# Expert layers of a routed network as seven block products instead of eight

## The chip, the core and the metric

The kernel runs on one core of a Trainium2 chip. Its engines work side by side, each through its own queue of instructions in order: TensorE (PE; its weight loads are shown apart as PEld), VectorE (DVE), ScalarE (ACT), GpSimd (POOL), and SyncE (SP), which here starts transfers. The metric is the device time of one execution in microseconds. Before the change the median of three runs is 1369.45 us (1367.98 to 1369.69).

## The reference

Four parts follow one another: a layer of experts, a linear attention in blocks, a conditioned attention, and two layers of local attention with a feed-forward part. The change touches the first alone. `x` has 4 x 512 tokens of 256 values, and there are eight experts.

```python
gate = xn @ wg_W + wg_b + (genre_embed @ gg_W + gg_b)
gate_w = jax.nn.softmax(gate, axis=-1)
topk_w, topk_i = jax.lax.top_k(gate_w, TOP_K)            # TOP_K = 2
cw = jnp.sum(jax.nn.one_hot(topk_i, E) * topk_w[..., None], axis=-2)
h1 = jax.nn.relu(jnp.einsum('bsh,ehm->bsem', x, W1) + b1)    # 256 -> 512
h2 = jax.nn.relu(jnp.einsum('bsem,emn->bsen', h1, W2) + b2)  # 512 -> 512
out_e = jnp.einsum('bsen,enh->bseh', h2, W3) + b3            # 512 -> 256
return jnp.einsum('bseh,bse->bsh', out_e, cw)
```

Everything is in 32-bit floats.

## The kernel before

Each token goes only to its two best experts. A first stretch computes the gate, sorts the 4096 pairs of token and expert by expert, and cuts them into slots of 256 or 128 rows; a slot has one expert, whose number is read from memory. `SLOTS` fixes the order: sizes 128, 256, 256, 128, 256, 256, then three times 128, 256, 256, 256, then 128, 256, 256, 128 (slots 0 to 21, of which fifteen have 256 rows), and two more of 128 that run only if they are needed. Rows that no token fills are written like the others, but to row 0 of the table `ys`, which nobody reads.

A slot `j` goes through these steps:

- `loads(j)`: SP starts three transfers of the expert's weights: `w1` (with its biases), `w2`, `w3`. There are two buffers for each.
- `gather(j)`: POOL issues one indirect transfer for each 128 rows, which fetches the tokens `xb`; TensorE transposes them into the bank `pxb`; ACT or DVE, in turn, copies them to `xbT`.
- `layer` with `w1`: result `h1`, 512 hidden units in four blocks of 128 partitions, tokens along the free side. For 256 rows that is 8 matmuls of 256 columns (two chunks of 128 inputs for each block). Two blocks share a PSUM bank, and ACT and DVE take turns at adding the bias and the relu (`relu`).
- `layer` with `w2`: result `h2`, from `h1`, 16 matmuls of 256 columns.
- `last(j)`: 8 matmuls with `w3` (4 for 128 rows) into `po`, one DVE addition of the bias into `ob`, and for each 128 rows an indirect transfer by POOL that scatters the rows to `ys`. A scatter waits until the scatter before it has landed.

The loop over the slots shifts these against one another: layer one of slot `j`, the last layer of slot `j - 1`, the loads, the gather and the transposes of slot `j + 1`, layer two of slot `j`. Except where code asks for program order (`PE.in_order`, `tc.keep_in_program_order`), a planner in the build sets the order on each engine from estimated times. Weights of later stages are loaded one by one in between (`later`), and POOL already adds bias rows (`crows`) to the residual tiles (`xres`) in this stage and clears a tile (`v`). When all slots are done, the results are read back from `ys`, weighted and summed into `y`, four tiles that nothing uses before.

PSUM has eight banks. In this stage four are for the layers (`mm`), two for transposes (`tp`), two for `po` and small products (`acc`). For the reader of the profile: a 32-bit matmul appears as two records, each with a weight load of its own; so the 16 matmuls of layer two of a 256-row slot are 32 records.

Of the kernel before, what the change touches and what calls it, by code (L numbers as in the profile page):

```python
# [12 lines left out]
F32 = mybir.dt.float32  # L13
I32 = mybir.dt.int32
AF = mybir.ActivationFunctionType
ALU = mybir.AluOpType
# [3 lines left out]
B, S, H = 4, 512, 256  # L20
NT = S // 128
# [21 lines left out]
NRARE = 2  # L43
NROWT = 2 * NPAIR + NHALF
NHI = 2 * NROWT
MCONST = (128, 128 + NE, 2 * NE, 2, NE * NE, NHI, 2 * B * NT, 64, NE)
NMC = sum(MCONST)


# [18 lines left out]
def adaln_attn_ffn_kernel(ctx: ExitStack, tc: tile.TileContext, a: dict, out: bass.AP):  # L68
# [50 lines left out]
    def acct(name):  # L119
        return bank("acc" if "acc" in ps_now else "mm", name)  # L120
# [1041 lines left out]
    with ExitStack() as abc:  # L1162
# [5 lines left out]


        with ExitStack() as moe:  # L1170
            moe.enter_context(banks("ps0", mm=4, tp=2, acc=2))
            xp = moe.enter_context(tc.tile_pool(name="xp", bufs=1, reuse_waits="tile"))
            ew = moe.enter_context(tc.tile_pool(name="ew", bufs=2, reuse_waits="tile"))
            hp = moe.enter_context(tc.tile_pool(name="hp", bufs=2, reuse_waits="tile"))
# [13 lines left out]
            for n in MCONST:  # L1188
                parts.append(mc[:, at : at + n])
                at += n  # L1190
            mtri, mtiles, mthr, mslot, mlow, miota, mtok, mfold, mwt = parts


            ys = dr.tile([1 + 2 * B * S, H], F32, tag="ys", name="ys")
            xall = a["x"].rearrange("b s h -> (b s) h")


# [8 lines left out]
            with PE.in_order():  # L1206

                warm = acct("pwarm")
                for _ in range(8):
                    PE.matmul(warm[:, 0:128], ident, ident, start=True, stop=True)  # L1210
                xT2s = [ew.tile([128, 4, ME], F32, tag="w2", name="xT") for _ in range(2)]
                xTs = [xT2s[b // 2][:, b % 2 * 2 + c, :] for b in range(B) for c in range(2)]

                for n, b in enumerate((0, 2, 3, 1)):
                    for c in range(2):
                        pt = mmt("pxt")
                        for t in range(NT):
                            PE.transpose(pt[:, t * 128 : (t + 1) * 128], xres[b][:, t, c * 128 : (c + 1) * 128], ident)
                        pinned(nc.vector.tensor_copy(xTs[2 * b + c], pt))
                    sq = hp.tile([128, NT, H], F32, tag="h2", name="sq")  # L1220
                    for t in range(NT):
                        nc.scalar.activation(sq[:, t, :], xres[b][:, t, :], AF.Square,
                                             accum_out=ss[:, b * NT + t : b * NT + t + 1])
                    if n == 1:

                        for c in range(2):
                            pinned(nc.vector.tensor_scalar_mul(wgs[:, c, 0:NE], wg[:, c, :], col("rms", c)))
                        csB = xp.tile([CD, B, 128], F32, tag="csB", name="csB")
                        pinned(nc.vector.tensor_copy(csB, csT.unsqueeze(2).to_broadcast([CD, B, 128])))
                        gb0 = xp.tile([128, NE], F32, tag="gb0", name="gb0")  # L1230
                        pinned(nc.vector.tensor_add(gb0, grow[:, 0, :], grow[:, 1, :]))
                pgb = acct("pgb")
                for b in range(B):
                    PE.matmul(pgb[:, b * NE : (b + 1) * NE], csB[:, b, :], ggw, start=True, stop=True)
                pg = acct("pg")
                for c in range(2):
                    for b in range(B):
                        PE.matmul(pg[32 * b : 32 * b + 32, :], wgs[:, c, :], xTs[2 * b + c],
                                  start=(c == 0), stop=(c == 1))
# [159 lines left out]
            pmap2 = acct("pmap2")  # L1399
            for q in range(2):  # L1400
                PE.matmul(pmap2[64 * q : 64 * q + 64, :NROWT], mfold, half_map[:, :, q], start=True, stop=True)
            goal = xp.tile([128, NROWT], I32, tag="goal", name="goal")
            nc.vector.tensor_copy(goal, pmap2[:, :NROWT])
            rowtok = xp.tile([128, NROWT], I32, tag="rowtok", name="rowtok")
            nc.vector.tensor_scalar(rowtok, pmap2[:, :NROWT], -1.0, 0.0, ALU.add, ALU.max)
            nc.vector.tensor_single_scalar(rowtok, rowtok, B * S - 1, op=ALU.bitwise_and)


            def busy(n):
# [7 lines left out]

            def relu(dst, src, bias):
                if turn[0]:
                    nc.scalar.activation(dst, src, AF.Relu, bias=bias)  # L1420
                else:
                    nc.vector.tensor_scalar(dst, src, bias, 0.0, ALU.add, ALU.max)  # L1422


            def place(kind, i):
# [11 lines left out]
                d.w3 = ew.tile([128, 5, H], F32, tag="w3", name="w3")  # L1437
                nc.sync.dma_start(d.w3, we[:, 8 + 6 * ME :].rearrange("p (c m) -> p c m", m=H))

            def gather(j, d):  # L1440
                xb = hp.tile([128, 2, H], F32, tag="xb", name="xb", bufs=3)
                for i in range(d.n):
                    r = place(d.n, SLOTS[j][0]) + i
                    nc.gpsimd.indirect_dma_start(
                        out=xb[:, i, :], out_offset=None, in_=xall,
                        in_offset=bass.IndirectOffsetOnAxis(ap=rowtok[:, r : r + 1], axis=0))
                n = d.n * 128
                pt = tpt("pxb")
                with PE.in_order():
                    for c in range(2):  # L1450
                        for i in range(d.n):
                            PE.transpose(pt[:, c * n + i * 128 : c * n + (i + 1) * 128],
                                         xb[:, i, c * 128 : (c + 1) * 128], ident)
                xbT = hp.tile([128, 2, 256], F32, tag="xbT", name="xbT")
                evac(xbT[:, :, 0:n], pt[:, : 2 * n].rearrange("p (c t) -> p c t", t=n))
                d.xbT = xbT

            def layer(d, src, tag, w, bias):
                n = d.n * 128
# [14 lines left out]
                        relu(dst[:, m, 0:n], ps[:, i * n : (i + 1) * n], d.w1[:, bias + m : bias + m + 1])  # L1474
                return dst

            def last(j, d):
                ps = acct("po")
                for i in range(d.n):
                    mm(ps[:, i * H : (i + 1) * H],  # L1480
                       [(d.h2[:, c, i * 128 : (i + 1) * 128], d.w3[:, c, :]) for c in range(4)])
                ob = hp.tile([128, 2, H], F32, tag="ob", name="ob", bufs=3)
                nc.vector.tensor_tensor(
                    ob[:, 0 : d.n, :], ps[:, : d.n * H].rearrange("p (i h) -> p i h", h=H),
                    d.w3[:, 4, :].unsqueeze(1).to_broadcast([128, d.n, H]), ALU.add)
                for i in range(d.n):
                    r = place(d.n, SLOTS[j][0]) + i
                    nc.gpsimd.indirect_dma_start(
                        out=ys, out_offset=bass.IndirectOffsetOnAxis(ap=goal[:, r : r + 1], axis=0),
                        in_=ob[:, i, :], in_offset=None)  # L1490


            later = {
# [5 lines left out]
            cond_weights(wp, lambda name, load: later.update({name: load}))  # L1499
            cw_ = {}  # L1500

            ds = [SimpleNamespace() for _ in SLOTS]
            loads(0, ds[0])
            gather(0, ds[0])
            often, rare = ds[:-NRARE], range(len(ds) - NRARE, len(ds))
            for j, d in enumerate(often):
                if j == len(often) - 1:
                    aside = conditions(cw_, wp)
                    next(aside)
                if j == len(often) - 2:  # L1510
                    halves = nc.values_load(nhalf[0:1, 0:1], min_val=0, max_val=2 * NE)
                if j == 1:
                    weights()
                h1 = layer(d, d.xbT, "h1", d.w1[:, 8:].rearrange("p (c m) -> p c m", m=ME), 0)
                if j:
                    last(j - 1, ds[j - 1])
                if j + 1 < len(often):
                    loads(j + 1, ds[j + 1])
                    gather(j + 1, ds[j + 1])
                    if j > 1 and later:  # L1520
                        name, behind[0] = next(iter(later)), True
                        cw_[name] = later.pop(name)()
                        behind[0] = False
                d.h2 = layer(d, h1, "h2", d.w2, 4)
            last(len(often) - 1, often[-1])

            next(aside)
            busy(1)
            with tc.If(halves > NHALF - NRARE):
                for j in rare:  # L1530
                    d = ds[j]
                    loads(j, d)
                    gather(j, d)
                    h1 = layer(d, d.xbT, "h1", d.w1[:, 8:].rearrange("p (c m) -> p c m", m=ME), 0)
                    d.h2 = layer(d, h1, "h2", d.w2, 4)
                    last(j, d)
            next(aside)
            busy(4)
            run(aside)
# [210 lines left out]
def _shape_constants():  # L1750
# [20 lines left out]
         np.tile((e[None, :] <= e[:, None]).reshape(-1), (128, 1)).astype(f), np.tile(np.arange(NHI), (128, 1)).astype(f),  # L1771
         (np.arange(2 * B * NT)[None, :] * 128 + p[:, None] + 1).astype(f),
         (p[:, None] % 64 == np.arange(64)[None, :]).astype(f),
         np.tile(np.where(e == NE - 1, 1 - NE, 1), (128, 1)).astype(f)], axis=1)

    pos = np.arange(S, dtype=f)
    inv = f(10000.0) ** np.repeat(np.arange(0, H, 2, dtype=f) / f(H), 2)
# [94 lines left out]
```

## Time and profile before

| | |
|---|---|
| median of three runs | 1369.45 us |
| the profiled execution, its own time | 1364.1 us |
| its span, first to last instruction | 1362.3 us |
| mean granted clock of TensorE | 0.990 |

The execution in stages, with each engine's busy time in each stretch. The columns are the stretch, its length, and for each engine its busy time and number of instructions; then the clock granted to TensorE, the share of DMA time and what it moved.

```profile
0.00:20.00 20.00, 12.18 (x76) 9.70 (x76) 9.37 (x25) 10.76 (x36) 3.62 (x14) 0.95 0.39 121
20.00:42.00 22.00, 11.87 (x85) 8.45 (x86) 14.81 (x56) 4.78 (x18) 3.19 (x4) 0.66 0.57 217
140.00:180.00 40.00, 40.00 (x218) 35.83 (x217) 8.60 (x18) 5.78 (x14) 12.00 (x14) 1.00 0.70 242
300.00:320.00 20.00, 19.18 (x95) 12.52 (x94) 6.87 (x22) 5.10 (x9) 3.07 (x5) 1.00 0.11 35
```

The five numbers with an x in parentheses are PE, PEld, DVE, ACT and POOL. The slots run from 42 to about 314 us; before 42 lies the gate and the sorting, after it the other three parts. In the slots the weights arrive at some 200 to 270 GB/s. Groups of instructions in later views are named by line, engine, operation and tiles (`out<-in`), with busy time, mean duration in ns, and the idle time before them with what ended it. Line 82 is the helper that issues every matmul, so groups are told apart by their tiles: `ph<-xbT,w` is layer one, `ph<-h,w` layer two, `po<-w,h` the last layer.

### The profile page before, as it was taken

What the parts mean: (1) busy time and instruction counts of PE and PEld (TensorE: products, weight loads), DVE (VectorE), ACT (ScalarE), POOL (GpSimd) and SP (SyncE); (2) the same over time, 40 slices, a digit from 0 to 9 for tenths busy, and PEclk for the clock granted to TensorE, in tenths of its full rate; (3) what the DMA queues carried; (4) which work ended last, traced back from release to release, by engine and by line L of the source; (5) the groups of instructions that cost most, each with busy time, mean ns of one, the idle gap of its engine ahead of it and who ended that gap; (6) DMA issues with size and microseconds to landing.
All of it is one profiled execution on the core that took longest, in us unless ns stands there. A gap on an engine that the chain in (4) does not pass through costs nothing.

```text
span 1362.3 us, 25766 instructions
## 1 busy us (share of the span) xinstructions
PE 1302.8 (96%) x10700; PEld 850.1 (62%) x10700; DVE 645.4 (47%) x1343; ACT 563.9 (41%) x1111; POOL 227.1 (17%) x223
## 2 busy tenths in 40 slices
PE   5899999998999999999999999999999998999998
PEld 4788888884666644444435665766555566667654
DVE  6222212125777743332226777764362767765421
ACT  4111111125555456565655646552223565463111
POOL 1324322211000020010103322100030312210010
PEclk7999999999999999999999999999999999999999
DMA  4577666644000000000201011211001011011000
GB/s 135 205 244 280 228 231 240 211 155 136 1 1 1 0 1 1 1 0 1 90 5 67 13 29 37 81 42 25 24 1 43 24 34 26 19 42 50 20 20 26
DMA packets 43110, 95.02 MB, mean 70 GB/s; under 512 B 9568, under 2 KB 25192, under 8 KB 40168
## 3 DMA queue, kind: packets, MB, share of 16 engines
q1 hardware_dynamic: 37560, 81.81, 18.1%
q0 software_dynamic: 3792, 10.24, 2.2%
q8 instruction: 88, 1.44, 0.4%
q10 hardware_dynamic: 1632, 1.21, 0.3%
q14 instruction: 38, 0.31, 0.1%
HBM read 83.95 MB, written 7.21 MB: 67 GB/s over the span
## 4 chain that ended last, share of the span: by engine, by line
PE 83%; DVE 7%; ACT 6%; issue 2%; DMA 1%; POOL 0%; POOLq 0%; SPq 0%; DVEq 0%; ACTq 0%
PE ph L82 14%; PE pdq L82 10%; PE sc L82 6%; PE pfy L82 6%; PE pug L82 5%; PE pua L82 5%; PE pv L82 5%; PE po L82 5%; PE pdy L82 4%; PE pn L82 3%; PE pz L82 2%; PE pds L82 2%; ACT p L685 2%; PE pqk L82 1%; PE pur L82 1%
## 5 line engine op out<-in xcount | busy, mean ns | idle before, releaser
L82 PE MATMUL pdq<-wqkv,yT 128*128 128x512 f32 x384 | 171.2, 596 | 6.0 <-ACT yT L613 4.1
L425 ACT ACTIVATE cex<-sc 128x512 f32<-128x512 f32 x256 | 131.8, 607 | 84.5 <-PE sc L82 84.4
L82 PE MATMUL ph<-h,w 128*128 128x256 f32 (+1 forms) x704 | 132.8, 346 | 1.6 <-DVE h L1422 1.6
L639 POOL TENSOR_TENSOR qr<-t,t 128x512 f32<-128x512 f32 x64 | 81.3, 1271 | 297.4 <-DVE t L636 282.8
L82 PEld LDWEIGHTS pdq<-wqkv,yT 128*128 128x128 f32 x384 | 71.4, 190 | 90.3 <-issue 76.9
L82 PEld LDWEIGHTS ph<-h,w 128*128 128x128 f32 x704 | 116.1, 191 | 13.7 <-DVE h L1422 1.9
L1420 ACT ACTIVATE h<-ph,w 128x256 f32<-128x256 f32 (+1 forms) x88 | 35.3, 437 | 190.9 <-PE ph L82 130.5
L1422 DVE TENSOR_SCALAR h<-ph,w 128x256 f32<-128x256 f32 (+1 forms) x88 | 36.1, 438 | 161.1 <-PE ph L82 102.6
L685 ACT ACTIVATE p<-pds,ss 128x192 f32<-128x192 f32 (+1 forms) x256 | 82.3, 434 | 12.5 <-PE pds L82 11.2
L82 PE MATMUL sc<-qm,kT 32*128 32x512 f32 x512 | 86.8, 639 | 0.0
L629 ACT ACTIVATE sq<-pdq 128x512 f32<-128x512 f32 x64 | 38.4, 601 | 97.1 <-POOL qr L639 50.2
L82 PE MATMUL pug<-hT,w 128*128 128x512 f32 x160 | 75.9, 597 | 0.0
L82 PE MATMUL pua<-hT,w 128*128 128x512 f32 x160 | 75.2, 592 | 0.0
L82 PE MATMUL ph<-xbT,w 128*128 128x256 f32 (+1 forms) x352 | 68.7, 347 | 0.5 <-ACT xbT L127 0.5
L82 PE MATMUL po<-w,h 128*128 128x256 f32 x296 | 67.6, 379 | 0.0
L395 POOL TENSOR_SCALAR fterm<-vw,faT 128x256 f32<-128x256 f32 x16 | 14.6, 922 | 312.1 <-DVE cr L385 259.6
L789 ACT ACTIVATE gl<-pug,cols 128x512 f32<-128x512 f32 x40 | 27.3, 687 | 86.5 <-PE pug L82 86.4
L82 PEld LDWEIGHTS ph<-xbT,w 128*128 128x128 f32 x352 | 58.5, 191 | 7.2 <-ACT xbT L127 0.7
L82 PE MATMUL pfy<-w,uA 128*128 128x256 f32 x256 | 61.2, 382 | 0.0
L82 PEld LDWEIGHTS pn<-p,v 64*64 64x64 f32 x1792 | 44.1, 136 | 27.4 <-issue 10.1
L82 PE MATMUL pv<-cex,v 128*32 128x512 f32 x512 | 61.2, 597 | 0.0
L82 PEld LDWEIGHTS po<-w,h 128*128 128x128 f32 x296 | 55.7, 190 | 8.1 <-ACT h L1420 0.9
(304 smaller groups left out, 2182.7 us busy)
## 6 DMA issues: line engine op xcount, KB each, us to landing
w<-in_moe_w_dram SPq DMA_DIRECT2D x22, 1024.0 KB
w<-in_moe_w_dram SPq DMA_DIRECT2D x22, 640.0 KB
w<-in_moe_w_dram SPq DMA_DIRECT2D x22, 516.0 KB
zb<-rows SPq DMA_DIRECT2D x32, 256.0 KB
g<-ys SPq DMA_DIRECT2D x6, 512.0 KB
wqkv<-in_f_wqkv_dram SPq DMA_DIRECT2D x2, 1536.0 KB
w<-in_f_w_dram SPq DMA_DIRECT2D x2, 1408.0 KB
out_dram<-yc SPq DMA_DIRECT2D x16, 128.0 KB
```

Of the source, the lines that this page charges most:

```text
L82: cls._queue(nc.tensor.matmul(*args, **kw))
L395: nc.gpsimd.tensor_scalar_mul(fterm[:, t, :], vw, W["faT"][:, t, b : b + 1])
L425: nc.scalar.activation(ex[:, i, :], pss[2 * j + i], AF.Exp, scale=CHD**-0.5)
L629: nc.scalar.activation(sq, p3, AF.Square)
L639: nc.gpsimd.tensor_tensor(qr_t[:, s], t1, t2, ALU.add)
L685: nc.scalar.activation(p[:, at : at + n], pss[j // 2][r][:, at % 384 : at % 384 + n], AF.Exp, scale=d.ss[:, j, 1, 2 * c + r : 2 * c + r + 1])
L789: nc.scalar.activation(gl, pg, AF.Gelu, bias=col("bg", l * (NU + 1) + i))
L1420: nc.scalar.activation(dst, src, AF.Relu, bias=bias)
L1422: nc.vector.tensor_scalar(dst, src, bias, 0.0, ALU.add, ALU.max)
```

## The change

For fourteen of the fifteen 256-row slots (all but slot 1) layers one and two are computed in another way. Weights are cut into 2 x 2 blocks (two halves of the inputs, two halves of the 512 outputs), the tokens' matrix also (two halves of the inputs, 128 and 128 rows). A product of such matrices takes eight block products; by a known identity (Strassen's, in Winograd's form) seven are enough, of sums of blocks on each side, whose results are then summed.

- The weights' side: `weight_sums`, four additions on POOL for each layer, 256 columns for layer one and 512 for layer two, into the `y` tiles, which are free in this stage. They are made for slot `j + 1` during slot `j`.
- The tokens' side: `token_sums`, four additions on DVE for each layer, on 128 columns for layer one and 256 for layer two. One operand of each is read from PSUM: for layer one the bank of the transposes; for layer two a tile of two banks (`act`), into which ACT writes three of the four blocks of `h1` a second time (`copies`).
- The products: `layer_few`, in the order p1, p2, p6, p5, p7, p4, p3. Each is two matmuls of 128 columns in layer one and four in layer two, so 14 and 28 instead of 8 and 16 of 256 columns.
- The results: ACT copies p1; DVE makes seven additions for each layer, each with a PSUM operand; ACT applies bias and relu to each of the four blocks in two halves of 128 columns.

Around this: PSUM is split into `mm` 4, `tp` 1, `acc` 1, `act` 2. The gather is cut into `fetch` (the transfers, now for slot `j + 2`) and `turn_tokens` (the transposes; the copy is always ACT's). All TensorE instructions of the slots, and those of the helpers, keep program order. The second scatter of a slot is issued after the first weight sums. Rows without a token get rows of their own behind the table (`maside`, `goalf`).

```diff
-            moe.enter_context(banks("ps0", mm=4, tp=2, acc=2))
+            moe.enter_context(banks("ps0", mm=4, tp=1, acc=1, act=2))
...
+            def turn_tokens(d):
+                n = d.n * 128
+                pt = tpt("pxb")
...
+                pinned(nc.scalar.copy(dst, src))
+                if d.few:
+                    d.t1 = token_sums(d.xbT, src)
...
+            def weight_sums(s, w):
...
+                pinned(nc.gpsimd.tensor_tensor(s[0], a21, a22, ALU.add))
+                pinned(nc.gpsimd.tensor_tensor(s[1], s[0], a11, ALU.subtract))
+                pinned(nc.gpsimd.tensor_tensor(s[2], a11, a21, ALU.subtract))
+                pinned(nc.gpsimd.tensor_tensor(s[3], a12, s[1], ALU.subtract))
...
+                b11, b12, b21, b22 = blocks(src)
+                _, c12, c21, c22 = blocks(src if psum is None else psum)
...
+                pinned(nc.vector.tensor_tensor(t[:, 0], c12, b11, ALU.subtract))
+                pinned(nc.vector.tensor_tensor(t[:, 1], c22, t[:, 0], ALU.subtract))
+                pinned(nc.vector.tensor_tensor(t[:, 2], c22, b12, ALU.subtract))
+                pinned(nc.vector.tensor_tensor(t[:, 3], c21, t[:, 1], ALU.subtract))
...
+                def block(i0, j0, out, p, other):
+                    plus(out, p, other)
+                    for m in range(2):
+                        pinned(nc.scalar.activation(
+                            dst[:, 2 * i0 + m, 128 * j0 : 128 * j0 + 128], out[:, m], AF.Relu,
+                            bias=d.w1[:, bias + 2 * i0 + m : bias + 2 * i0 + m + 1]))
+                    if copies is not None and (i0, j0) != (0, 0):
+                        for m in range(2):
+                            pinned(nc.scalar.activation(
+                                copies[:, 2 * i0 + m, 128 * j0 : 128 * j0 + 128], out[:, m], AF.Relu,
+                                bias=d.w1[:, bias + 2 * i0 + m : bias + 2 * i0 + m + 1]))
...
+                p1 = product(whole(0, 0), src[:, 0:n, 0:128])
+                pinned(nc.scalar.copy(e1, p1))
+                p2 = product(whole(0, 1), src[:, n : 2 * n, 0:128])
+                block(0, 0, e15, p2, e1)
+                p6 = product(summed(1), t[:, 1])
+                plus(e16, p6, e1)
+                p5 = product(summed(0), t[:, 0])
+                plus(e15, p5, e16)
+                p7 = product(summed(2), t[:, 2])
+                plus(e17, p7, e16)
+                block(1, 1, e16, p5, e17)
+                p4 = product(whole(1, 1), t[:, 3])
+                block(1, 0, e1, p4, e17)
+                p3 = product(summed(3), src[:, n : 2 * n, 128:256])
+                block(0, 1, e15, p3, e15)
...
+                with PE.in_order():
+                    if d.few:
+                        copies = both_banks()
+                        h1 = layer_few(d, d.xbT, d.t1, "h1", w1, d.s1, 0, copies)
+                        t2 = token_sums(h1, copies)
+                    else:
+                        h1 = layer(d, d.xbT, "h1", w1, 0)
+                    if j + 1 < len(often):
+                        loads(j + 1, after)
...
+                    if after.few and j + 2 < len(often):
+                        fetch(j + 2, ds[j + 2])
+                    if j:
+                        last(j - 1, ds[j - 1])
+                        scatter(j - 1, ds[j - 1], 0)
+                    if after.few:
+                        first_sums(after)
+                    elif j + 2 < len(often):
+                        fetch(j + 2, ds[j + 2])
+                    if j:
+                        scatter(j - 1, ds[j - 1], 1)
+                    if j + 1 < len(often):
+                        turn_tokens(after)
+                    d.h2 = layer_few(d, h1, t2, "h2", d.w2, d.s2, 4) if d.few else layer(d, h1, "h2", d.w2, 4)
+                if after.few:
+                    second_sums(after)
```

## The prediction

> **What bounds the kernel now.** I read the page first: TensorE's share, the slices, the chain that ended last. Then the stretch of the expert slots (42 to 312 us), TensorE's timeline in it, its groups with shapes kept apart, and POOL's timeline.
>
> ```profile
> PE 1302.8 (96%) x10700; PEld 850.1 (62%) x10700; DVE 645.4 (47%) x1343; ACT 563.9 (41%) x1111; POOL 227.1 (17%) x223
> PE   5899999998999999999999999999999998999998
> PE 83%; DVE 7%; ACT 6%; issue 2%; DMA 1%; POOL 0%; POOLq 0%; SPq 0%; DVEq 0%; ACTq 0%
> L82 PE MATMUL ph<-h,w 128*128 128x256 f32 (+1 forms) x704 | 132.8, 346 | 1.6 <-DVE h L1422 1.6
> ```
>
> The expert layers (`ph`) are TensorE's largest group on the chain, and TensorE waits 1.6 us in all for their inputs. Cut by windows, TensorE is busy 40.00 of every 40 us from 60 to 300, at a granted clock of 1.00. So a microsecond of matmul saved there is a microsecond, as long as nothing else becomes late. What an instruction costs is its pitch, start to start:
>
> ```profile
> 149.13 3.62 PE L82 MATMUL ph<-xbT,w 128*128 128x256 f32 x16
> 152.58 3.62 PE L82 MATMUL po<-w,h 128*128 128x256 f32 x16
> 156.03 0.38 PE L86 MATMUL pxb<-ident,xb 128*128 128x128 f32 x2
> 156.25 7.07 PE L82 MATMUL ph<-h,w 128*128 128x256 f32 x32
> 163.16 1.95 PE L82 MATMUL ph<-xbT,w 128*128 128x128 f32 x16
> 164.94 3.62 PE L82 MATMUL po<-w,h 128*128 128x256 f32 x16
> ```
>
> Each f32 matmul is two records. A 256-row slot takes 3.45 us (152.58 - 149.13) for layer one, 3.45 for the previous slot's last layer, 0.22 or 0.44 for transposes, 6.91 for layer two: 216 ns a record of 256 columns. A 128-row slot shows 128-column records: 1.78 / 16 = 111.5 ns. With the previous slot also of 256 rows a period is 14.26 us if the next has 256 rows, 14.04 if 128; after a 128-row slot (its last layer 1.73) it is 12.54, 12.32.
>
> **TensorE's part of the change.** In 14 slots the 16 + 32 records of 256 columns become 7 products each: 28 + 56 records of 128 columns.
> - Before: 48 x 0.216 = 10.37 us. After: 84 x 0.1115 = 9.37. Saved: 1.0 us a slot, **14.1 us** in all.
> - Against it stands a rule of the Trainium skill, "TensorE: Matmul & The Clock Gate", Back-to-back issue gap: in a stream of weight loads and matmuls, 128 columns cost about 81 ns a matmul instead of 56, since weight loads no longer hide. Taking a record as two passes, the estimate is 162 ns x 84 = 13.6 us: a loss of 3.2 us a slot, 45 in all. The 128-row slot has the same weights and the same 128 columns; its weight loads fill the stretch (PEld 3.60 of 3.60 us) and its records still come every 111.5 ns. I take the row: at the edge, not over it.
>
> **The helpers' part.** Here the change pays. Per changed slot it removes 8 relus and adds on ACT 2 copies and 22 relus (8 + 6 into PSUM + 8), on DVE 14 sums with a PSUM operand and 4 + 4 token sums, on POOL 8 weight sums. The rows nearest:
>
> ```profile
> L1483 DVE TENSOR_TENSOR ob<-po,w 128x256 f32<-128x256 f32 x6 | 2.5, 425 | 6.8 <-PE po L82 6.8
> L127 ACT COPY xbT<-pxb 128x256 f32<-128x256 f32 x5 | 1.9, 372 | 24.9 <-PE pxb L86 24.9
> L1420 ACT ACTIVATE h<-ph,w 128x128 f32<-128x128 f32 x28 | 10.3, 367 | 61.5 <-PE ph L82 31.7 <-DVE h L1422 18.5 <-issue 11.2
> L396 POOL TENSOR_TENSOR fterm<-fterm,crows 128x256 f32<-128x256 f32 x16 | 11.3, 725 | 0.0
> L639 POOL TENSOR_TENSOR qr<-t,t 128x512 f32<-128x512 f32 x64 | 81.3, 1271 | 297.4 <-DVE t L636 282.8 <-PE pdy L82 13.5 <-PE pds L82 1.0
> 29.59 1.06 ACT L1390 ACTIVATE ol<-ol,mc 128x64 f32<-128x64 f32 x4 [8.63 <-DVE ol L1381]
> ```
>
> The last line: four scalings of 336 ns (64 columns, SBUF to SBUF, a column operand) in 1.06 us, so they overlap by 0.095. I take 0.39 us for a relu from SBUF (336 ns + 64 columns at 0.83 ns, the slope of ACT's copies between 256 and 512 columns), 0.365 into PSUM (the 367 row has the opposite direction; no row has this one, bounds 0.30 and 0.39), 0.30 and 0.27 when one follows another without a wait; for DVE 0.42 (0.33 directly behind another, whose overlap is 0.09), 0.29 at 128 columns. Hand-over between DVE and ACT 0.04, from a matmul to a reader 0.25, back to TensorE 0.06, all read off the timeline.
>
> First 256-row slot behind a 128-row one (five of them), from the start of layer one:
> - p1 done 0.45, its copy done 1.7 (ACT still has relus of the small slot); first sum and two relus to 2.9; then three sums in a row, since the first of them rewrites the tile that the relus read: 4.1.
> - ACT then has 12 activations, 3.9 us: 8.05. Six of them are the copies into PSUM.
> - Token sums of layer two begin only then, as the first needs the last block: the second, which p6 reads, is done at 8.96.
> - TensorE reaches p6 at 3.12 + 1.73 + 0.44 + 2 x 0.89 = 7.1. It **waits 1.9 us**; then five products, 4.46: the slot ends at 13.5 instead of 12.54. 0.96 x 5 = **+4.8**.
>
> A 256-row slot behind another (eight): a loop of ACT and DVE closes over the slot, because both queues are in order. Copy 0.3; sum, two relus, three sums 2.5; 12 activations 3.9; four token sums 1.5; `ob` 0.6; layer-one sums of the next slot 0.9; layer two's sum, relus, three sums 2.4; its last six relus 1.9: **14.0 us**, against 13.25 of matmuls. Slack from the small slots is eaten first; I take 13.8: 3 x (13.8 - 14.26) + 5 x (13.8 - 14.04) = **-2.6**. The first changed slot stands behind an unchanged 256-row slot, whose last layer (3.45) covers the token sums: TensorE's 1.0 is kept, **-1.0**.
>
> So the stage's fourteen slots come to +1.2, not -14.1: the gain becomes waits. With no overlap it would be +24 (a slot has about 25 of them, 0.09 each, and most lie in the loop: some 1.7 us a slot); with relus at 0.367 it is -2.6.
>
> **POOL.** Per slot in a run: two gathers and two scatters at 1.27 (0.97 and 0.30 of issue), weight sums 4 x 0.73 and 4 x 1.27: 13.1 us of 13.8. The second scatter waits for the first to land; that took 2.5 to 2.9 us between 256-row slots and is covered by the first weight sums (2.95); near small slots 3.5 to 5.2, with slack. DVE is not in POOL's way: the sums have one SBUF operand each, and `t<-pdq,tab` takes 414 ns beside POOL's `qr`, while operations with two wait for it (2.62 us for two below).
>
> ```profile
> 322.84 2.62 DVE L1558 SCALAR_TENSOR_TENSOR ymoe<-g,m,g 128x256 f32<-128x256 f32 x2 [0.37 <-ACT g L1557]
> 322.44 2.34 POOL L1579 TENSOR_TENSOR xres<-xres,crows 128x1024 f32<-128x1024 f32 x1 [5.20 <-DMA g<-ys]
> 127.62 6.98 POOL L1579 TENSOR_TENSOR xres<-xres,crows 128x1024 f32<-128x1024 f32 x3
> 134.54 1.80 POOL L311 MEMSET v<- 128x2048 f32 x1
> ```
>
> One thing has lost its cover. Three additions for a later stage and a memset (the last two lines; 9.1 us with a small memset) lie in POOL's queue, today beside idle time. In the changed program they stand in slot 7, behind slot 9's gathers and ahead of slot 6's scatter and slot 8's first weight sums. In slot 6, of 9.24 us, the previous `ob` comes at 6.2; scatter 1.3, sums 2.9, scatter 1.3, slot 7's larger sums 5.2: POOL is done with these 7.6 us into slot 7. Then gathers 2.5, the aside 9.1, the scatter 1.3, two sums 1.5: the sum that slot 8's p6 reads comes at 22.0, and TensorE is there at 13.5 + 0.9 = 14.4. **+7.5**, once.
>
> **The rest.** Order pinned: slot 0 and 1 no longer interleave; layer two of slot 0 can start behind the transposes instead of at 46.87: -0.9. At the end `acc` has one bank, so the four small `pcs` products and `pfp`, which today lie between matmuls, wait for DVE in turn ahead of slot 21: +2. The extra DVE operation for `goal` stands behind `rowtok`'s first: 0. Gathers moved ahead, rows without a token written to rows of their own, weights loaded by SP in the same order: 0, as the loads have over a slot's time (bounds -1 and +3).
>
> **Sum**: +1.2 + 7.5 + 2 - 0.9 = **+9.8 us**, say +9.5. The profiled execution took 1364.1 us (its span 1362.3), so 1373.6 on its scale; the shown median, 1369.45, lies 5.3 above, so **1379**.
>
> **Rivals.**
> - Helpers keep up: the loop falls under 13.2 us and the token sum is there by 7.1 us, so TensorE waits only for POOL's aside: -14.1 + 7.5 + 1.1 = -5.5, **1364**. For it: DVE and ACT have about 10 us of work each in 13.5. Against it: the loop is a chain, not a share. It decides from 0.8 us off the loop on. Chance 0.16.
> - No overlap behind waits: most added activations carry a wait. +24 in the slots, +8.6 for the rest: +32, **1401**; half of it 1390. Against it: ACT's `ex` operations overlap by 0.1 though they wait for TensorE. Chance 0.2.
> - POOL becomes the bound: scatters land in 5 us in every slot, as in the worst pair but one; then 1.27 + 5 + 1.27 + 5.1 + 2.5 = 15.2 a slot, some +12 more: **1391**. Chance 0.1.
> - Weight loads show (the rule above): +45, **1415**. Chance 0.03.
> - The forecast, 0.51, 1368 to 1388 by itself.
>
> The range reaches from the first rival to the second, 1362 to 1400; outside it lie half of the second, the fourth and a third of the first. A measurement can tell 0.2% (2.7 us) from no change. Faster: 0.16 + 0.01 from the forecast's lower edge; within 0.2%: 0.08; slower: 0.75.
>
> **What shows it.** Records of `ph` at 111.5 ns; TensorE idle in front of products of `ymoe` tiles (p6 of layer two) in every slot behind a small one; one idle of about 7 us in front of slot 8's products, released by POOL; POOL busy 9 tenths. It is wrong if TensorE's share in the stage stays at 100% (faster), or if its idle is put to POOL in every slot.

## The result, and the profile after

The changed kernel takes 1392.97 us (median of four runs, 1389.99 to 1394.6), the kernel before 1368.95 in the runs beside it: 1.0176 times as long, 95% interval 1.0155 to 1.0198. That is some 24 us more, where the forecast said 9.5. The profiled execution has a span of 1390.8 us.

The page's busy times, TensorE's slices of the span and its granted clock:

```profile
PE 1301.2 (94%) x11204; PEld 862.1 (62%) x11204; DVE 723.6 (52%) x1585; ACT 653.2 (47%) x1402; POOL 337.5 (24%) x335
PE   5989699998999999999999989999999998999998
PEclk7999899999999999999999999999999999999999
PE 60%; DVE 6%; ACT 6%; issue 3%; DMA 2%; POOL 0%; SPq 0%; POOLq 0%; ACTq 0%; DVEq 0%
```

TensorE has 504 more records and is busy 1.6 us less. A slice is 35 us long. The fifth, 139 to 174 us, falls from 9 tenths to 6, and its clock digit to 8; the third falls from 9 to 8. POOL's 0% in the chain is no acquittal: the shares shown add up to 77% of the span, so almost a quarter has no name there. TensorE's list of waits in the stage (42 to 345 us) gives the names: who was waited for, microseconds in total, times, the longest.

```profile
PE ph L82 <- POOL ymoe L1501: 21.1, 8, 11.3
PE ph L82 <- DVE ymoe L1519: 5.5, 9, 1.1
PE pxb L86 <- DMA xb<-in_x_dram,rowtok: 1.1, 1, 1.1
```

L1501 is the second weight sum, which p6 reads; L1519 the second token sum. Before, TensorE's waits in front of `ph` were one of 1.6 us for DVE and one of 0.5 for ACT. Now POOL alone costs it 21.1 us, half of that in one place, slot 8. TensorE's timeline there (start, duration, operation, records, idle before it):

```profile
136.00 1.06 PE L82 MATMUL ph<-ymoe,w 128*128 128x128 f32 x8
136.89 1.06 PE L82 MATMUL ph<-h,ymoe 128*128 128x128 f32 x8
137.78 1.06 PE L82 MATMUL ph<-xbT,w 128*128 128x128 f32 x8
150.17 2.93 PE L82 MATMUL ph<-t,ymoe 128*128 128x128 f32 x12 [11.33 <-POOL ymoe L1501]
152.89 1.06 PE L82 MATMUL ph<-t,w 128*128 128x128 f32 x4
```

From 136.00 to 137.78 sixteen records start in 1.78 us, 111 ns each: the price on which TensorE's gain was reckoned. Behind the idle of 11.33 us twelve records take 2.72 us, double that. The windows view gives the granted clock for the 6 us from 150 (columns: stretch, length, TensorE busy and records, clock, DMA share, GB/s):

```profile
150.00:156.00 6.00, 5.83 (x26) 0.57 0.01 3
```

So the idle costs another 2.6 us (an estimate: 6.0 x 0.43) in slow matmuls. And POOL's own queue ahead of that sum:

```profile
117.15 1.00 POOL L1592 DMA_INDIRECT ys<-ob,goal  x1 [2.46 <-DMA ys<-ob,goal]
...
123.07 1.01 POOL L1592 DMA_INDIRECT ys<-ob,goal  x1 [2.40 <-issue]
...
126.28 0.73 POOL L1503 TENSOR_TENSOR ymoe<-w,ymoe 128x256 f32<-128x256 f32 x1
129.50 1.00 POOL L1592 DMA_INDIRECT ys<-ob,goal  x1 [2.49 <-DMA ys<-ob,goal]
...
134.35 1.27 POOL L1503 TENSOR_TENSOR ymoe<-w,ymoe 128x512 f32<-128x512 f32 x1
...
138.03 6.93 POOL L1712 TENSOR_TENSOR xres<-xres,crows 128x1024 f32<-128x1024 f32 x3
144.91 1.79 POOL L311 MEMSET v<- 128x2048 f32 x1
...
147.53 1.02 POOL L1592 DMA_INDIRECT ys<-ob,goal  x1 [0.56 <-issue]
...
149.39 0.72 POOL L1501 TENSOR_TENSOR ymoe<-ymoe,w 128x256 f32<-128x256 f32 x1
```

Read it from the end. The sum that slot 8 needs stands behind the additions, as the prediction said. But the additions start late, and why is seen further up: each scatter waits for the one before it to land, which at 129.50 was 5.4 us after that one's issue was over (124.08). The sums queued behind such a scatter wait too. Slot 6's layer one begins at 114.30; the prediction had POOL done with slot 7's sums 16.8 us later, and it is done at 135.6, 21.3 us later.

Where the 24 us arise: the last `pbusy` before the next part starts at 321.8 us before and at 344.2 after. So 22.4 of the profile's 28.5 us lie in the expert stage, and 21.2 of these between the starts of slot 2 and slot 20 (two lines of before, two of after):

```profile
63.25 3.62 PE L82 MATMUL ph<-xbT,w 128*128 128x256 f32 x16
285.07 3.62 PE L82 MATMUL ph<-xbT,w 128*128 128x256 f32 x16
62.28 1.05 PE L82 MATMUL ph<-xbT,w 128*128 128x128 f32 x8
305.35 1.06 PE L82 MATMUL ph<-xbT,w 128*128 128x128 f32 x8
```

The parts nearly add up. The records of the thirteen changed slots in between save 13.0 us, at 1.0 each. Against that stand 21.1 us of waits for POOL, 5.3 for DVE and 2.6 of slow clock. Each of these 16 waits also costs about 0.26 us beyond its idle (in slot 4 the next record comes 3.06 us late behind an idle of 2.90, and the twelve records behind it take 1.44 us instead of 1.34), some 4 us together. That is 20 of the 21.2.

The later 6.1 us come for the most part in two places that the change does not touch (1.6 between the first `pck` and the first `pv` of the conditioned attention, 4.0 between the first `pdq` and the first `pug`). In each the changed kernel's granted clock is at a half for 3.4 us (from 503.3 and from 813.9), where the profile of before has no such stretch; by an estimate that is worth 1.7 us each (half of 3.4). The medians differ by less than the two profiles do.

### The profile page after: what moved, and what is told of

It is laid out like the page before. It is cut to its first block, busy times and chain, and to the rows that moved or that the text cites. A ratio compares the mean times of both kernels' runs of the same rounds, so it can differ in the third digit from the quotient of the medians.

```text
span 1390.8 us, 27510 instructions
## 1 busy us (share of the span) xinstructions
PE 1301.2 (94%) x11204; PEld 862.1 (62%) x11204; DVE 723.6 (52%) x1585; ACT 653.2 (47%) x1402; POOL 337.5 (24%) x335
## 3 DMA queue, kind: packets, MB, share of 16 engines
q8 instruction: 92, 1.51, 0.5%
## 4 chain that ended last, share of the span: by engine, by line
PE 60%; DVE 6%; ACT 6%; issue 3%; DMA 2%; POOL 0%; SPq 0%; POOLq 0%; ACTq 0%; DVEq 0%
PE pdq L82 9%; PE sc L82 6%; PE pfy L82 6%; PE pug L82 5%; PE pua L82 5%; PE pv L82 5%; PE pdy L82 4%; PE pn L82 3%; PE pz L82 2%; PE pds L82 2%; ACT p L685 2%; PE pqk L82 1%; PE pck L82 1%; PE pf L82 1%; PE pur L82 1%
## 5 line engine op out<-in xcount | busy, mean ns | idle before, releaser
L1549 ACT ACTIVATE h<-e,w 128x128 f32<-128x128 f32 x224 | 75.1, 391 | 94.6 <-DVE e L1559 94.3
L1559 DVE TENSOR_TENSOR e<-ph,e 128x256 f32<-128x256 f32 x196 | 76.2, 419 | 48.0 <-PE ph L82 31.0
L82 PE MATMUL ph<-h,w 128*128 128x128 f32 (+1 forms) x480 | 61.1, 283 | 0.0
L82 PE MATMUL pn<-p,v 64*64 64x128 f32 (+1 forms) x1792 | 50.5, 252 | 11.2 <-DVE p L688 8.9
L1592 POOL DMA_INDIRECT ys<-ob,goal x37 | 36.8, 995 | 96.3 <-DVE ob L1584 48.1
L630 DVE TENSOR_REDUCE ss<-sq 128x8 f32<-128x512 f32 x64 | 43.5, 679 | 31.5 <-ACT sq L629 31.5
```

The lines of the kernel that those rows point to most:

```text
L82: cls._queue(nc.tensor.matmul(*args, **kw))
L630: nc.vector.reduce_sum(ss[:, t, s, :], sq, axis=AX.X)
L1549: pinned(nc.scalar.activation(dst[:, 2 * i0 + m, 128 * j0 : 128 * j0 + 128], out[:, m], AF.Relu, bias=d.w1[:, bias + 2 * i0 + m : bias + 2 ...
L1559: pinned(nc.vector.tensor_tensor(out, p, other, ALU.add))
L1592: pinned(nc.gpsimd.indirect_dma_start(out=ys, out_offset=bass.IndirectOffsetOnAxis(ap=goal[:, r : r + 1], axis=0), in_=d.ob[:, i, :], in_o ...
```

## The experiments

The theory was: POOL is the excess. Its queue is in order, and in it scatters wait for a landing and the additions run for 9 us, with weight sums behind them that TensorE needs. Rivals: the round through ACT and DVE, the new frame (pinned order, banks, moved gathers), and, later, the PSUM copies. All times are medians; the ratio, with its 95% interval, is against the kernel before in the same runs (1366.5 to 1367.8 us; 1368.95 beside the changed kernel). Differences named below are between medians. The kernel before ran 1.1 to 2.5 us slower beside the changed kernel than beside the others, and differences from the changed kernel are uncertain by as much.

| kernel | us | ratio | interval |
|---|---|---|---|
| changed kernel | 1392.97 | 1.0176 | 1.0155 to 1.0198 |
| e1, additions behind the stage | 1383.25 | 1.0127 | 1.0081 to 1.0173 |
| e2, sums ahead of scatters | 1381.32 | 1.0097 | 1.0070 to 1.0123 |
| e3, both | 1376.54 | 1.0060 | 1.0040 to 1.0080 |
| e4, frame without products | 1371.43 | 1.0033 | 1.0018 to 1.0048 |
| e5, e3 without weight sums | 1376.27 | 1.0074 | 1.0048 to 1.0099 |
| e6, e3 without PSUM copies | 1366.22 | 0.9988 | 0.9977 to 0.9998 |
| e7, e3 with ACT's order changed | 1369.23 | 1.0012 | 1.0002 to 1.0023 |
| e8, e7 with additions spread, end mended | 1363.81 | 0.9972 | 0.9956 to 0.9987 |
| e9, e8 without PSUM copies | 1360.18 | 0.9956 | 0.9938 to 0.9974 |
| e10, changed kernel without PSUM copies | 1386.75 | 1.0130 | 1.0098 to 1.0162 |

### The additions taken out of the slots

```diff
-                nc.gpsimd.tensor_tensor(
-                    xres[b], xres[b], row("bo").unsqueeze(1).to_broadcast([128, NT, H]), ALU.add)
+                pinned(nc.gpsimd.tensor_tensor(
+                    xres[b], xres[b], row("bo").unsqueeze(1).to_broadcast([128, NT, H]), ALU.add))
```

Pinned, the additions stay behind the stage, and the memset with them.

> The three additions to xres and the memset of v (9.1 us of POOL) are pinned behind the expert slots; nothing else moves. POOL theory: the stall of 11.3 us ahead of slot 8's p6 goes, and with it the low clock after it (some 2.5 us): -14, about 1379 us; the stalls of 1.1 to 2.9 us behind other slots stay (about 10 us in all). Rival, the loop of ACT and DVE sets the slots' pace: it takes the place of the stall, and no more than 7 us go. Rival, the frame (pinned order, banks, moved gathers) costs the time: less than 3 us go.

Measured: 9.7 us less than the changed kernel, 4 short of the forecast, and with an interval that overlaps the changed kernel's; so the trace has to decide. Slot 8's stall is 0.57 us, and TensorE still waits 9.8 us for POOL in seven places. `pcs`, the first of the small products ahead of slot 21, starts 12.5 us earlier, so the stage itself gained most of the 14 forecast. Part is given back behind it, where POOL's additions now lie beside DVE's weighting of `y`, whose operations have two SBUF operands: two of them take 5.00 us, where the profile of before had 2.62, and TensorE's first transposes wait 4.7 us instead of 2.35.

### Weight sums ahead of the scatters

```diff
                         last(j - 1, ds[j - 1])
-                        scatter(j - 1, ds[j - 1], 0)
                     if after.few:
                         first_sums(after)
...
                     if j:
-                        scatter(j - 1, ds[j - 1], 1)
+                        scatter(j - 1, ds[j - 1], 0)
...
                 if after.few:
                     second_sums(after)
+                if j:
+                    scatter(j - 1, ds[j - 1], 1)
```

> On POOL the weight sums stand ahead of the scatters (first scatter behind layer one's sums, second behind layer two's), so no sum waits for a scatter to land; the additions stay in slot 7. POOL theory: the stalls of 1.1 to 2.9 us on POOL's sums go (-9.8 us), and slot 8's of 11.3 shrinks by the 4.4 us by which POOL came late to it: -10 to -14, 1379 to 1383 us. Rival, the additions alone are the excess and the small stalls are replaced by ACT and DVE: less than 5 us go. Rival, later scatters hold up POOL's gathers instead: no gain.

Measured: 11.7 us less than the changed kernel, with the additions still in slot 7. Every small stall on the second weight sum is gone (a single new one of 1.4 us waits for the first sum), and slot 8's has halved:

```profile
141.04 2.93 PE L82 MATMUL ph<-t,ymoe 128*128 128x128 f32 x12 [5.38 <-POOL ymoe L1501]
```

So the landing of scatters made the small stalls and about half of the large one. Its twelve records are as slow as behind 11.33 us of idle (2.72 us to the next group's start at 143.76).

### Both

> Both edits: no additions in the slots, sums ahead of scatters. POOL theory: all 21 us of POOL stalls and the 2.5 us of low clock go: -23, about 1370 us, which is the time before; what is left of the saving on TensorE is then lost to ACT and DVE and to the end of the stage. Rival, ACT and DVE set the pace: 1379 to 1385 us. Should the two edits do more than each of them summed, slot 7's delay had been counted twice.

Measured: 16.4 us less than the changed kernel, where 23 were forecast. TensorE never waits for POOL in the stage; its largest wait there is

```profile
PE ph L82 <- DVE ymoe L1519: 8.1, 10, 1.4
```

The two edits give less than their sum (21.4 us), since each shortens the same stall in slot 8. The stage ends (last `pbusy`) 18.3 us earlier than in the changed kernel, but the additions behind the stage cost again, here 2.6 us ahead of the first `pqk` against the kernel without the products below. And DVE's waits grew from 5.5 to 8.1 us: part of what POOL gave free went to the round through ACT and DVE.

### The frame without the products

```diff
-            ds = [SimpleNamespace(few=n == 2 and j > 1) for j, (_, n) in enumerate(SLOTS)]
+            ds = [SimpleNamespace(few=False) for j, (_, n) in enumerate(SLOTS)]
```

> No slot uses the seven products; the pinned order, the banks, the moved gathers and scatters, and the rows of their own for rows without a token stay. By the prediction's steps: -0.9 (head) +2.6 (end of the stage): +1.7 over before, about 1371 us. Rival, the frame carries the excess: 1380 us or more. If the second scatter's wait for the first holds up gathers, TensorE waits for xb: 1375.

Measured: 3.6 us over before (every gather stands behind the first scatter here, as there are no sums to make). So the frame is not where the 24 us are. The additions hold up POOL here too, though there are no sums: gathers are late instead, and TensorE waits in slot 8 for the next slot's tokens:

```profile
142.46 0.76 PE L86 MATMUL pxb<-ident,xb 128*128 128x128 f32 x4 [1.65 <-DMA xb<-in_x_dram,rowtok]
```

Slots 7 and 8 are 2.4 us longer than before. The stretch of slot 20 and the small products behind it grows from 15.11 to 17.43 us, as predicted for one `acc` bank.

### Without weight sums

The eight sums are replaced by plain blocks of the weights (`s[:] = [a21, a11, a12, a22]`), on top of both edits.

> e3_both with the eight weight sums of a slot left out: the products that should read a sum of weight blocks read a plain block of the weights, so POOL does only gathers and scatters. Theory: in e3_both POOL is off the path, so the time stays within 2 us of it (1375 to 1378 us), and so do the slots' periods (13.6 to 13.9 us): ACT and DVE set them. Rival, POOL still holds TensorE or slows DVE: 4 us or more go, 1372 us or less.

Measured: the time stays at 1376.27 us, and every period from slot 2 to slot 19 agrees with that of the kernel with both edits to 0.02 us. With POOL's queue mended, its work costs nothing; the waits that are left in front of the second layer are for DVE's token sums (8.4 us, ten times; 8.1 with the weight sums).

### Two ways at the round of ACT and DVE

In the kernel with both edits, a slot behind a small one looks so (slot 4, layer one's end and layer two's beginning):

```profile
89.64 0.69 ACT L1549 ACTIVATE h<-e,w 128x128 f32<-128x128 f32 x2 [1.28 <-DVE e L1559]
90.24 0.75 ACT L1554 ACTIVATE ph<-e,w 128x128 f32<-128x128 f32 x2
90.93 0.68 ACT L1549 ACTIVATE h<-e,w 128x128 f32<-128x128 f32 x2
91.52 0.76 ACT L1554 ACTIVATE ph<-e,w 128x128 f32<-128x128 f32 x2
92.21 0.68 ACT L1549 ACTIVATE h<-e,w 128x128 f32<-128x128 f32 x2
92.80 0.75 ACT L1554 ACTIVATE ph<-e,w 128x128 f32<-128x128 f32 x2
93.58 0.42 DVE L1518 TENSOR_TENSOR ymoe<-ph,h 128x256 f32<-128x256 f32 x1 [3.31 <-ACT ph L1554]
94.04 0.42 DVE L1519 TENSOR_TENSOR ymoe<-ph,ymoe 128x256 f32<-128x256 f32 x1
94.61 2.92 PE L82 MATMUL ph<-ymoe,ymoe 128*128 128x128 f32 x24 [1.37 <-DVE ymoe L1519]
```

Twelve ACT operations without a gap, 3.9 us; DVE stands idle for 3.31 us and starts the token sums when the last is over, and TensorE waits. Six of the twelve (L1554) are the copies into PSUM. One experiment leaves them out, the other only moves four operations behind the ones that are read first:

```diff
-                        copies = both_banks()
-                        h1 = layer_few(d, d.xbT, d.t1, "h1", w1, d.s1, 0, copies)
-                        t2 = token_sums(h1, copies)
+                        h1 = layer_few(d, d.xbT, d.t1, "h1", w1, d.s1, 0)
+                        t2 = token_sums(h1)
```

> e3_both without the result written to PSUM: six ACT operations of 0.35 us fewer a slot, and layer two's token sums take two SBUF operands. If DVE reads two SBUF operands freely beside POOL, the token sums start 2.1 us earlier and the five waits of 1.4 us go: 1369 us. If such sums wait for POOL's operations, as additions of two SBUF operands did for 1.3 us each beside xres in the profile of before, four sums cost 1.9 to 3.6 us more and the wait grows by up to 1.5 us a slot: 1385 to 1395 us. The second is forecast, 1386.

```diff
...
+                    if copies is not None and i0 == j0 == 1:
+                        relus(copies, i0, j0, out)
+                    elif copies is not None and j0 == 1:
+                        relus(copies, i0, j0, out)
+                        relus(dst, i0, j0, out)
+                        relus(copies, 1, 0, e1)
+                        relus(dst, 1, 1, e16)
+                    else:
+                        relus(dst, i0, j0, out)
...
```

> e3_both with ACT's twelve results of a layer in another order: those that the token sums read (the PSUM copies of two blocks, and the block that the second product reads) ahead of the four that are read later. Same work. Theory: the chain through ACT in the slots behind a small one is what holds p6, by 1.4 us; four operations (1.4 us) fewer stand ahead of the token sums, the five waits go: -6.5, about 1370 us, and the periods behind a small slot fall from 13.6 to 12.2. Rival, the round of ACT and DVE as a whole sets the pace (all of their work in a slot): less than 2 us go.

Measured: the new order gave 7.3 us less than with both edits alone, about as forecast; but the period behind a small slot fell to 13.01 only, not 12.2, and the five waits to 0.8 us. The other slots gained as well (13.1 to 13.6 us).

Leaving the copies out gave 10.3 us less, where I had expected 9.5 more. Why, in the same slot:

```profile
88.04 1.87 ACT L1549 ACTIVATE h<-e,w 128x128 f32<-128x128 f32 x6 [1.28 <-DVE e L1559]
89.83 1.00 POOL L1592 DMA_INDIRECT ys<-ob,goal  x1 [0.15 <-DMA w<-in_moe_w_dram]
89.94 0.43 DVE L1518 TENSOR_TENSOR ymoe<-h 128x256 f32<-128x256 f32 x1 [1.27 <-ACT h L1549]
...
91.47 2.84 PE L82 MATMUL ph<-ymoe,ymoe 128*128 128x128 f32 x24
```

ACT is done in half the time, the sums start 1.90 us after ACT began on the blocks instead of 3.94, and p6 waits for nothing. The sums have two SBUF operands and still take 0.43 us, since POOL is issuing a scatter and not adding. They do meet POOL's sums in three of the fourteen slots (8, 12 and 16), for instance at

```profile
137.52 1.51 DVE L1520 TENSOR_TENSOR ymoe<-h 128x256 f32<-128x256 f32 x1
138.01 0.73 POOL L1500 TENSOR_TENSOR ymoe<-w 128x256 f32<-128x256 f32 x1
```

where four sums take 3.7 us instead of 1.6. The Trainium skill, "SBUF — State Buffer" (Terms), says that DVE and POOL share a pair of ports by an exclusive lock, held for the full instruction, and that the loser blocks. The 1.51 us agree with it. How often the two meet depends on the order of POOL's queue: in the kernel of the next section, whose queue is not mended, the four sums take 2.5 to 5.4 us in nine of the fourteen slots.

### The changed kernel with only the copies undone

> The changed kernel with one part undone: no copies in PSUM, POOL's queue as it was. POOL theory: its stalls (21 us) stay and only DVE's waits go: -5, 1388 us. Rival, the copies are the excess by themselves: -10 or more as in e6_no_psum_copies against e3_both, 1383 us or less.

Measured: 6.2 us less than the changed kernel, or 3.8 when each is taken against the kernel before in its own runs; the two intervals overlap. From slot 2 to slot 20 the profile is 5.4 us shorter. TensorE still waits 9.7 us for POOL's sum in slot 8, but the forecast that all 21 us of POOL's stalls would stay was a miss: POOL's waits come to 10.5 us in three places. Instead TensorE waits 9.6 us for DVE (5.5 in the changed kernel), whose token sums now meet POOL's weight sums, for instance in slot 4:

```profile
92.44 1.34 POOL L1501 TENSOR_TENSOR ymoe<-ymoe,w 128x512 f32<-128x512 f32 x1
92.69 1.37 DVE L1519 TENSOR_TENSOR ymoe<-h,ymoe 128x256 f32<-128x256 f32 x1
```

Even so the stage is faster without the copies. They are a part of the excess, not the excess.

### A version that beats both

The additions are spread over slots 9, 13 and 17, at whose end POOL has no weight sums to make; `pcs` takes `mm` banks and `pfp` goes behind slot 21's layer one.

```diff
+                if j in (9, 13, 17):
+                    pinned(add_bo((9, 13, 17).index(j) + 1))
...
-            ps = acct("pcs")
+            ps = mmt("pcs")
...
+                    if j == len(often) - 1:
+                        next(aside)
```

> e7_copies_first, with the additions to xres spread over three slots ahead of a small one (where POOL has no weight sums), and pcs in the mm banks with pfp behind layer one of the last slot. Expected against e7_copies_first: -2.5 at the first transposes behind the stage (DVE no longer waits beside the additions), -2.3 at the last slot; about 1366 us, some 2 below before. If spread additions hold POOL up again: stalls of 1 to 2 us in slots 11, 15 and 19, and no gain.

Measured: 5.4 us less than e7, 0.28% below before. The stretch of slot 20 and the small products is 14.32 us (16.32 without this edit, 15.11 before), and the first transposes wait 2.4 us instead of 4.5. No wait for POOL appears.

> e8_all_mended without the copies in PSUM (ACT's order as in the changed kernel, its six added operations gone): the slots' periods as in e6_no_psum_copies (11.98 behind a small slot, 13.1 to 13.7 otherwise), the last slot and the first transposes as in e8_all_mended. e6 was 3.7 us ahead of e8 where the small pcs products start, so 1360 us, 7 to 8 below before. If the gain of e6 does not add to e8's, 1363.

Measured: 1360.18 us (1358.8 to 1362.91), 6.3 us below the kernel before, and as forecast. Only slots 12 and 16 take longer than was said (14.0 us, said 13.7 at most): there the four token sums take 4.2 us beside POOL's. Its page:

```profile
PE 1291.8 (95%) x11204; PEld 856.3 (63%) x11204; DVE 730.4 (54%) x1585; ACT 629.0 (46%) x1318; POOL 339.8 (25%) x335
PE   4999999999999999999999899999999998999998
```

POOL does as much as in the changed kernel (339.8 against 337.5 us busy) and TensorE waits for none of it. The products' arithmetic was worth having, if little: 0.4%. What it lost lay in the order of the queues around it and in the copies.

## Where the prediction was right, and the step that failed

**TensorE, -14.1: right.** Records of 128 columns come every 111 ns between waits, though 84 of them with as many weight loads follow one another in a slot. The rule that would have made them 162 ns does not show.

**ACT and DVE, +1.2: right.** The costs taken from neighbouring rows came out: a relu from SBUF takes 391 ns (said 0.39 us), one into PSUM 361 (said 0.365), a DVE sum 419 (said 0.42). The sum of them could only be seen with POOL out of the way. With both edits the slots behind a small one take 13.59 us (said 13.5), the others behind a 256-row slot 13.65 to 13.93 (said 13.8), slot 2 13.10 against 14.03 (said -1.0). Summed from slot 2 to slot 19, that is about +2.

**Head and end: right.** Slot 2 starts 1.0 us earlier than before (said 0.9); the stretch of slot 20 is 1.7 us longer in the changed kernel and 2.3 in the frame alone (said 2). A slow clock behind the small products, which was not forecast, comes on top (last section).

**POOL, +7.5 once: the term that failed.** It measured 21.1 us of waits and 2.6 us of slow clock, 23.7 in place of 7.5. That is 16 us more, and the forecast missed by 14.5. The order of the queue was read rightly (the additions ahead of slot 8's sum); what the sum had at nothing were the waits for scatters to land near small slots ("with slack") and the slow clock. Three things were in it:
- The prediction read scatters as landing in 2.5 to 2.9 us between 256-row slots and in 3.5 to 5.2 near small ones, "with slack". In the changed kernel the median from 60 to 290 us is 4.7 us from issue to landing, 3.7 from the end of the issue, as the prediction counted. The slack was not there: the scatters ahead of the late sums near the small slots start 5.9 to 7.9 us after the ones before them. The slack of a small slot had been counted from the time when `ob` is ready (6.2 us into slot 6); the scatter started 8.8 us into it, 4.9 us after the issue of its predecessor was over. Sums queued behind such scatters held TensorE by 1.1 to 2.9 us, six times in layer one and once in layer two: 9.8 us in all.
- The same delay moved the additions: 11.33 us in slot 8, not 7.5. Both are shown by the sums moved ahead of the scatters, which took away the former and half of the latter.
- Behind the idle of 11 us TensorE ran at a mean clock of 0.57 for 6 us, which the sum did not have.

The rival that made POOL the bound (+12 on top, 1391 us) came nearest in time, but not in its mechanism: POOL was not full. From 60 to 290 us it is busy 156.7 of 230 us in the changed kernel and 167.7 with both edits, which is faster. The prediction's own sign, POOL busy 9 tenths, did not show either: 156.7 of 230 is 7 tenths.

What the prediction also missed is the copies' own worth. It counted them (six of twelve in the chain of 3.9 us) but took the freedom from POOL that they buy as needed. Without them the stage is faster, with POOL's sums where they are.

The prediction also read TensorE's waits for `ph` before as 1.6 us in all; 0.5 us for `xbT` belongs to them. Nothing hangs on it.

One thing stays open: why landings near small slots take longer. Weights are being loaded then, but no run changed the loads alone. Nor is all explained that happens behind the stage: from the first `pqk` to the end the profiles last from 1035.6 us (before) to 1047.4 (e7). In that stretch TensorE worked at half the clock for some 5 us before and some 25 in e7, which makes about 10 of these 12 us by an estimate from those lengths. Part of it follows the additions behind the stage: from the first `pqk` to the first `pck` it is 124.8 us in e3 and e7, which have them there, and 121.8 in the changed kernel. For the other stretches the cause is not shown.

## What to carry to other kernels

Work added to an in-order queue inherits every wait that is ahead of it in that queue: list those waits with their measured durations, and put what the bounding engine needs ahead of what waits for a transfer. Count a chain by its instructions on each engine before paying extra instructions to avoid a conflict, and look in the timeline whether the conflicting operations would meet at all. An engine that is busy for two thirds of a stage can still be what holds it up.

## What the hardware showed beyond that

A stall can cost more than its own length, by the granted clock. Behind an idle of 2.90 us (slot 4) the next twelve records took 1.44 us, near the usual pace. Behind 5.38 us (e2) and behind 11.33 us twelve records took 2.72, and the clock stood at 0.57 for 6 us each time: some 2.6 us beyond the idle itself, by the estimate above. That alone agrees with the Trainium skill, "TensorE: Matmul & The Clock Gate" (HAM oscillation — how this bites in real kernels), which puts the limit for idle gaps at about 3.4 us.

But shorter gaps were followed by a low clock too. Ahead of slot 21 no idle is longer than 0.45 us, and yet layer one's sixteen records start 3.35 us ahead of the next group instead of 1.78, and the granted clock from 322.40 to 325.80 is 0.50 (changed kernel):

```profile
321.19 1.03 PE L82 MATMUL pfp<-cwe,hdT 128*4 128x256 f32 x4 [0.45 <-DVE hdT L244]
322.14 3.56 PE L82 MATMUL ph<-xbT,w 128*128 128x128 f32 x16
325.49 3.79 PE L82 MATMUL po<-w,h 128*128 128x256 f32 x16
```

In the kernel before it is 0.50 from 325.3 to 328.7 us, right behind a wait of 2.35 us. So the length of one idle does not decide it: 2.90 us in slot 4 were free of it and 2.35 us there were not. What does decide it no run here shows.
